# Last expert layer of a graph network on one Trainium2 core: the inner values are kept in DRAM as token rows and gathered, instead of being computed a second time

## The chip, the cores and the metric

The kernel runs on one core of a Trainium2 chip. The metric is the time of one execution in microseconds (us). Three runs of the kernel before the change took 1784.53, 1791.91 and 1784.44 us; their median is 1784.53 us. One further execution was taken with the profiler.

The core has five engines, and the text calls them by their short names: TensorE (PE, with its weight loads as PEld), VectorE (DVE), ScalarE (ACT), GpSimd (POOL) and SyncE (SP). Each works through its own list of instructions in order, and semaphores tie the lists together. SP, ACT and POOL issue the transfers between DRAM and the on-chip memory (SBUF); TensorE writes its results into another on-chip memory (PSUM), from which DVE or ACT must copy them out.

## What is computed

The model has two layers over 2500 nodes (tokens) with 256 features. Each layer adds a graph convolution, an attention block and a layer of experts. Only the last part of the second layer changes, a layer of eight experts of which each token uses the one that its gate likes best:

```python
def _L1_ffn_ref(x, W1, b1, Wg, bg, Wd, bd):
    xf = x.reshape(-1, orig_shape[-1])
    H = jax.nn.gelu(xf @ W1 + b1, approximate=False)        # 2500 x 1024
    probs = jax.nn.softmax((H @ Wg + bg) / TEMP, axis=-1)   # 2500 x 8
    assign = jnp.argmax(probs, axis=-1)
    out = jnp.zeros_like(xf)
    for e in range(Wd.shape[0]):
        y = H @ Wd[e] + bd[e]                               # 1024 -> 256
        sel = (assign == e)[:, None]
        out = out + jnp.where(sel, probs[:, e:e + 1] * y, 0.0)
    return out.reshape(orig_shape)
...
x = x + _L1_ffn_ref(_layernorm(x, axis=-1)[None], L1_ffn_W1, L1_ffn_b1, L1_ffn_Wg, ...)[0]
```

The inner values `H` are the same for all experts: they depend on the token alone. They are needed twice, once for the gate and once for the product with the down weights `Wd[e]` of the token's expert.

## The kernel before

All arithmetic is in float32. The trace shows two instructions of TensorE for each float32 product in the text, and one for each transpose. The 2500 tokens are 20 tiles of `P` = 125, in `NG` = 5 groups of `GT` = 4 tiles (`GC` = 500 tokens). `X` holds the rows on chip; a row has `RW` = 260 numbers: 256 features, then the mean and the inverse deviation of its norm (columns `D` and `D + 1`), the gate's probability (`D + 2`) and the token's number (`D + 3`).

**Gating** (`layernorm_T` at L1899 with `gates`, L1838) goes over the five groups. DVE normalises four tiles into `lnt`, TensorE turns them (L482, eight transposes a group), and the copies of `evacuate` (L98), which alternate between ACT and DVE, put them into `xTf`. For each of eight slices `j` of 128 inner values, TensorE multiplies with `w1` (L1851, four instructions of 500 columns) and ACT applies GELU (L1854) into `h`, one of eight buffers. `logits` multiplies four slices at a time with the gate's weights (L1845). `route` (L1866) turns the logits into probabilities, chooses the expert, and counts where each token's row goes in a sorted table in DRAM; POOL then scatters the rows into `sorted1` and, for the first three groups, also into `early1` (L547, one indirect DMA a tile, by addresses in `to`). `route` is a generator, and its two later parts run within the next group, after slices 2 and 5. The inner values `h` of a group are dropped when the logits are done.

At the head of this stage SP loads the gate's weights and the down weights `wd` of all experts, eight loads of 1 MB (L1733).

**The first four tiles** are full tiles of experts that are known after three groups. `whole_tiles` (L1757) finds them, SP loads their rows from `early1` into `xe` (L1793), DVE normalises them (`turned_first`, L1795), and `hidden_first` (L1802) computes their inner values with the same product and GELU (L1808, L1809) into `he`, while the last group's routing ends. `visit_first` (L1813) multiplies with the down weights.

**The visits** take the other 2000 tokens, in 16 tiles of 128 sorted rows (the last has 80). A tile may hold tokens of several experts, and so there are `NV` = 23 visits, one for each pair of a tile and an expert. `visits` (L620) computes the lists that say which tile and which expert a visit has; they are read into registers at run time. The 16 tiles are handled in groups of 2, 2, 4, 4 and 4:

- `fetch` (L1950) has POOL gather the rows of each tile from `sorted1` into `xs` (L1953; `xs` is `X`, used again), by addresses in `whence`.
- `turned` (L1958) normalises a group's rows a second time on DVE (L1965, `xh`), turns them on TensorE (L1967, `px`), and copies them into `xc`.
- `inner` (L1973) multiplies with `w1` a second time (L1978) and applies GELU on ACT (L1980, and L1983 for the last, short tile) into `hs`, a ring of `RING` = 12 tiles.
- `take` (L1985) copies a visit's tile out of the ring on DVE (L1990), its place being known only at run time.
- `visit` (L1993) multiplies it with the expert's down weights, 16 instructions of 256 columns (L2000, into `py`, of which there are two), makes the list of output rows (L2004, L2005), adds bias, probability and the residual row (L2007, L2008, into `yo`), and has POOL scatter the rows into the output (L1831, in `written`). It reads its row of `xs` at an index from a register (`ds(r, 1)`).

The framework derives what an instruction must wait for from the regions that instructions read and write, in the order of the text; a region at a run-time index counts as the whole. It also fixes each engine's order when the kernel is built, near to the order of the text but not equal to it.

Products in progress take their PSUM tiles from `mm_tile` (L86, four of them). `weights` (L682) hands out tiles of 128x2048 from `wpool`, which has two (L1164); `w1` is one of them.

Of the kernel before, what the change touches and what calls it, by code (L numbers as in the profile page):

```python
# [66 lines left out]
def gps_kernel(ctx: ExitStack, tc: tile.TileContext, a, out):  # L67
# [30 lines left out]
    def evacuate(dst, src):  # L98

        flip[0] ^= 1  # L100
        if flip[0]:
            S.copy(dst, src)  # L102
        else:
            V.tensor_copy(dst, src)
# [602 lines left out]
    early1 = dram.tile([NE // 2 * N, RW], F32, name="early1")  # L707

# [1003 lines left out]
    with ExitStack() as last:  # L1712
# [82 lines left out]
        def turned_first():  # L1795

            t = fin2.tile([P, GT, D], F32, tag="lnt", name="lnt")
            for k in range(GT):
                V.tensor_scalar(t[:, k, :], xe[:, k, :D], xe[:, k, D:D + 1], xe[:, k, D + 1:D + 2], ALU.subtract, ALU.mult)
            transpose_group(xT, 0, lambda k: t[:, k, :])  # L1800

        def hidden_first():  # L1802

            next(routing[-1])
            for j in range(nj):
                ps = mm_tile(128, GC)
                for c in range(2):
                    T.matmul(ps, w1[:, c, j * 128:(j + 1) * 128], xT[:, c, 0:GC], start=(c == 0), stop=(c == 1))  # L1808
                S.activation(he[:, j, :], ps, AF.Gelu, bias=b1f[:, j:j + 1])  # L1809
                if j == 3:  # L1810
                    next(routing[-1])
# [26 lines left out]
        def gates(g):  # L1838
# [9 lines left out]
            for j in range(nj):  # L1848
# [5 lines left out]
                S.activation(hh[j], ps, AF.Gelu, bias=b1f[:, j:j + 1])  # L1854
                if j == 5:
                    logits(0)
# [37 lines left out]
        def sort_all():  # L1894
            V.tensor_copy(fill1, begin1.rearrange("p k t -> p (k t)"))
            moved.append([])
            moved1.append([])
            routing.clear()
            layernorm_T(X, xT, lambda g: fin2.tile([P, GT, D], F32, tag="lnt", name="lnt"), stats=with_row, then=gates)  # L1899
            hidden_first()  # L1900
# [41 lines left out]
        groups = []  # L1942
        for n in (2, 2, 4, 4, 4):
            lo = groups[-1][1] if groups else 0
            groups.append((lo, lo + n))
# [4 lines left out]
        def fetch(lo, hi):  # L1950
            for t in range(lo, hi):
                m = rows_of(t)
                G.indirect_dma_start(  # L1953
                    out=xs[:m, t, :], out_offset=None, in_=sorted1,
                    in_offset=bass.IndirectOffsetOnAxis(ap=whence[:m, t:t + 1], axis=0),
                )

        def turned(lo, hi):  # L1958

            xc = fin2.tile([128, 2, 4 * TS], F32, tag="xc", name="xc")  # L1960
            ps = [psum2.tile([128, 4 * TS], F32, tag="ag", name="px") for c in range(2)]
            for t in range(lo, hi):
                m = rows_of(t)
                xh = fin2.tile([128, D], F32, tag="xh", name="xh", bufs=4)
                V.tensor_scalar(xh[:m], xs[:m, t, :D], xs[:m, t, D:D + 1], xs[:m, t, D + 1:D + 2], ALU.subtract, ALU.mult)  # L1965
                for c in range(2):
                    T.transpose(ps[c][:, (t - lo) * TS:(t - lo) * TS + m], xh[:m, c * 128:(c + 1) * 128], ident[:m, :m])  # L1967
            n = min(hi * TS, LATER) - lo * TS
            for c in range(2):
                evacuate(xc[:, c, :n], ps[c][:, :n])  # L1970
            return xc, n

        def inner(lo, hi, xc, n):  # L1973
            s = lo % RING
            for j in range(nj):
                ps = mm_tile(128, 4 * TS)
                for c in range(2):
                    T.matmul(ps[:, :n], w1[:, c, j * 128:(j + 1) * 128], xc[:, c, :n], start=(c == 0), stop=(c == 1))  # L1978
                k = n // TS
                S.activation(hs[:, s:s + k, j * TS:(j + 1) * TS], ps[:, :k * TS].rearrange("p (k t) -> p k t", t=TS), AF.Gelu,  # L1980
                             bias=b1f[:, j:j + 1])
                if n % TS:
                    S.activation(hs[:, s + k, j * TS:j * TS + n % TS], ps[:, k * TS:n], AF.Gelu, bias=b1f[:, j:j + 1])  # L1983
# [27 lines left out]
        fetch(*groups[0])  # L2011
        fetch(*groups[1])
# [81 lines left out]
```

## Time and profile before

| What | us |
|---|---|
| median of three runs | 1784.53 |
| the profiled execution's own time | 1791.08 |
| its span, from first to last instruction | 1789.4 |
| granted TensorE clock in it, mean | 0.98 |
| L1851, products of gating, begin | 1517.06 |
| one group of gating, from the products of one (1574.63) to those of the next (1593.42) | 18.8 |
| L1822, products of the first four tiles | 1628.01 to 1642.06 |
| L2000, products of the visits, end | 1784.01 |

An execution's time is a little longer than its span, here by 1.7 us. "Busy" is time in which an engine had an instruction under way. In a timeline, a line gives the start, the length, the engine, the line of the kernel, the operation, what it writes and reads, its shape, and how many instructions are merged in it; in brackets stands the idle time of the engine just before it, and what ended it. The modelled end of a TensorE instruction lies after the start of the next one, so its pace is read from the differences of starts. A windows line gives a stretch's start and end, its length, the busy time of PE, PEld, DVE, ACT and POOL with their instructions, the granted clock, the share of the DMA engines' time and the bytes moved in GB/s.

### The profile page before, as it was taken

How to read it: one execution, taken by the hardware profiler on the slowest of the kernel's cores; microseconds unless marked ns; L12 is line 12 of the kernel's file. 1: busy time of each engine (PE TensorE's matmuls, PEld its weight loads, DVE VectorE, ACT ScalarE, POOL GpSimd, SP SyncE). 2: the span in 40 equal slices, each digit the busy share in tenths (PEclk: the TensorE clock that was granted, in tenths of full speed). 3: DMA queues.
4: the chain of work that ended last, by engine and by line, in shares of the span. 5: the costliest groups of instructions: out<-in, count | busy, mean ns of one | idle time of the engine just before them, and what ended most of it. 6: DMA issues, size and time to landing. Idle time of an engine off the chain costs nothing. (4 is left out here: it accounts for less than half of the span.)

```text
span 1789.4 us, 24685 instructions
## 1 busy us (share of the span) xinstructions
PE 1709.2 (96%) x8081; PEld 1252.7 (70%) x8081; DVE 1011.2 (57%) x2909; ACT 654.4 (37%) x1170; POOL 947.7 (53%) x942
## 2 busy tenths in 40 slices
PE   4889998999899999999999999999999999998998
PEld 3656666989778667687776787767877767446767
DVE  7677743434555567577567276575665646234323
ACT  5743322323541434343433524334434331442220
POOL 2003474456207777777774657777777610243222
PEclk7899998999899999999999999999999999999999
DMA  5121147868537534555444764545543312521100
GB/s 143 42 77 37 35 139 244 252 216 236 138 89 183 98 92 112 153 159 172 126 124 118 199 110 146 139 126 152 160 138 97 86 51 75 185 60 48 34 20 29
DMA packets 131653, 216.59 MB, mean 121 GB/s; under 512 B 32832, under 2 KB 97526, under 8 KB 131259
## 3 DMA queue, kind: packets, MB, share of 16 engines
q0 software_dynamic: 51264, 111.78, 23.1%
q1 hardware_dynamic: 77947, 99.17, 18.5%
q10 hardware_dynamic: 2304, 3.94, 0.9%
q8 instruction: 70, 1.15, 0.3%
q14 instruction: 68, 0.56, 0.1%
HBM read 169.44 MB, written 47.79 MB: 121 GB/s over the span
## 5 line engine op out<-in xcount | busy, mean ns | idle before, releaser
L1321 POOL DMA_INDIRECT piece<-tab,nbr x574 | 595.4, 1037 | 188.1 <-issue 155.5
L1638 PE MATMUL mm<-w,h 128*125 128x256 f32 x1280 | 288.8, 379 | 2.0 <-ACT h L1630 1.9
L1627 PE MATMUL mm<-xT,w 128*128 128x500 f32 x640 | 282.1, 582 | 0.0
L1638 PEld LDWEIGHTS mm<-w,h 128*125 128x125 f32 x1280 | 237.7, 188 | 46.3 <-issue 8.5
L1627 PEld LDWEIGHTS mm<-xT,w 128*128 128x128 f32 x640 | 119.1, 190 | 111.0 <-issue 104.3
L1630 ACT ACTIVATE h<-mm,bf 128x500 f32<-128x500 f32 x160 | 106.5, 675 | 202.0 <-PE mm L1627 201.7
L1333 DVE TENSOR_TENSOR piece<-piece 128x1024 f32<-128x1024 f32 (+3 forms) x130 | 146.6, 1129 | 20.6 <-DMA piece<-tab,nbr 20.2
L465 PE MATMUL pa<-edges,xb 125*128 125x500 bf16 x600 | 141.0, 387 | 5.5 <-DVEq L961 3.6
L465 PEld LDWEIGHTS <-xb 125*128 125x128 bf16 x600 | 59.3, 102 | 69.9 <-issue 14.0
L1033 POOL DMA_INDIRECT back<-yo,xs x60 | 60.1, 1002 | 85.9 <-DVE yo L1031 43.6
L1640 DVE TENSOR_TENSOR tok<-tok,mm 125x256 f32<-125x256 f32 x80 | 33.4, 418 | 116.4 <-PE mm L1638 116.3
L1595 DVE TENSOR_TENSOR tok<-tok,po 125x256 f32<-125x256 f32 x80 | 30.1, 417 | 115.4 <-PE po L1592 115.0
L494 ACT ACTIVATE tok<-tok,less,rstd 125x256 f32<-125x256 f32 x140 | 72.1, 590 | 56.3 <-DVE less L492 56.3
L1016 PE MATMUL mm<-xc,wt 128*128 128x128 f32 x688 | 86.9, 281 | 5.5 <-DVE xc L1007 5.5
L811 ACT CAST edges<-mm 125x500 bf16<-125x500 f32 x100 | 65.0, 790 | 71.4 <-PE mm L808 71.4
L1020 ACT ACTIVATE h<-mm,wt 128x128 f32<-128x128 f32 x172 | 49.2, 367 | 106.0 <-issue 84.9
L1016 PEld LDWEIGHTS mm<-xc,wt 128*128 128x128 f32 x688 | 82.7, 196 | 6.3 <-DVE xc L1007 6.2
L1026 PE MATMUL py<-w,h 128*128 x344 | 84.0, 388 | 0.2 <-ACT h L1020 0.2
L2000 PE MATMUL py<-wd,taken 128*128 x368 | 80.9, 379 | 0.5 <-DVE taken L1990 0.5
L1517 PE MATMUL mm<-wa,xT 128*125 128x256 f32 x320 | 76.9, 394 | 4.6 <-ACT xT L487 3.9
L1289 PE MATMUL da<-t,e 125*125 125x256 f32 x320 | 77.7, 379 | 0.0
L2000 PEld LDWEIGHTS py<-wd,taken 128*128 128x128 f32 x368 | 69.7, 190 | 11.3 <-issue 1.4
(486 smaller groups left out, 2995.9 us busy)
## 6 DMA issues: line engine op xcount, KB each, us to landing
wt<-in_expert_in_dram SPq DMA_DIRECT2D x43, 514.0 KB
sorted<-nothing SPq DMA_DIRECT2D x8, 1269.5 KB
piece<-tab,nbr POOLq DMA_INDIRECT x574, 3.1
e<-adj SPq DMA_DIRECT2D x40, 218.8 KB
w<-in_L_mix_W_dram SPq DMA_DIRECT2D x8, 1024.0 KB
wd<-in_L_ffn_Wd_dram SPq DMA_DIRECT2D x8, 1024.0 KB
t<-tab SPq DMA_DIRECT2D x20, 224.0 KB
adj<-wide SPq DMA_DIRECT2D x20, 218.8 KB
```

What stands on the lines that cost most here:

```text
L465: T.matmul(pa[c], table[:, k, n, c * 128:(c + 1) * 128], edges[:, k, :], start=(k == 0 and n == 0), stop=(k == NT - 1 and n == 2))
L494: S.activation(rows[:, k, :D], src[:, lo + k, :D], AF.Identity, bias=less[:, k:k + 1], scale=rstd[:, k:k + 1])
L1016: T.matmul(ps[:, j * TS:(j + 1) * TS], wt[:, c * F0 + j * 128:c * F0 + (j + 1) * 128], xc[:, c * TS:(c + 1) * TS], start=(c == 0), stop=(c ...
L1026: T.matmul(ps, h[:, j * TS:(j + 1) * TS], w2[:, ds(e, 1), j, :], start=(j == 0), stop=(j == NJ - 1))
L1289: T.matmul(sums[d // 2][:, d % 2, :], e[:, d * P:(d + 1) * P], t[:, k, :], start=(i + k == 0 and d % 2 == 0), stop=(i + k == NT - 1 and d ...
L1321: G.indirect_dma_start(out=t[:, i, :], out_offset=None, in_=tab, in_offset=bass.IndirectOffsetOnAxis(ap=by, axis=0))
L1333: V.tensor_tensor(total[:, :m, :], total[:, :m, :], t[:, :m, :], ALU.add)
L1517: T.matmul(ps[:, k * D:(k + 1) * D], hT[:, c, (i + k) * P:(i + k + 1) * P], wk[:, c, :], start=(c == 0), stop=(c == 1))
L1627: T.matmul(ps, w1[:, c, j * 128:(j + 1) * 128], fT[:, c, g * GC:(g + 1) * GC], start=(c == 0), stop=(c == 1))
L1630: S.activation(h, ps, AF.Gelu, bias=bf[:, l, j:j + 1])
L1638: last["product"] = T.matmul(ps, hh[j][:, k * P:(k + 1) * P], w2[:, j, :], start=(j == 0), stop=(j == nj - 1)).ins
L2000: T.matmul(ps, h[:, j * TS:(j + 1) * TS], wd[:, ds(e, 1), j, :], start=(j == 0), stop=(j == nj - 1))
```

## The change

The inner values that gating computes are not dropped. Four slices at a time (a half, `n`), TensorE turns them back into token rows, one tile of 125 tokens after another (`keep_half`, four transposes into one PSUM tile); ACT or DVE copies them into `hr`, one of three buffers, and SP stores them into a new table `inners` in DRAM, 2500 rows of 1024 numbers. `move` (L92) makes two DMA issues of each store. The tiles to be kept wait in a list, `keeping`, from which one is taken after each GELU of `gates` and of `hidden_first`. To make room, `lnt` and `lT` have one buffer instead of two.

In the visits the second norm, its transposes, the second product with `w1` and the second GELU are gone. A tile's rows are gathered from `sorted1` as before, now one tile at a time; DVE makes the token numbers into integers (`ids`); and with them POOL gathers the tiles' inner values from `inners` (`fetch_inner`, 128 rows of 4 KB, into a half of a `weights` tile). `inner` turns them back with eight transposes, and two copies put them into the ring. The loop runs over visits, with the stages two, four and six tiles ahead, in place of groups.

```diff
+    inners = dram.tile([N, F1], F32, name="inners")
...
-            t = fin2.tile([P, GT, D], F32, tag="lnt", name="lnt")
+            t = fin2.tile([P, GT, D], F32, tag="lnt", name="lnt", bufs=1)
...
+        def keep_half(g, n, k, hh):
+
+            ps = mm_tile(P, 4 * 128)
+            for q in range(4):
+                T.transpose(ps[:, q * 128:(q + 1) * 128], hh[q][:, k * P:(k + 1) * P], ident)
+            hr = fin2.tile([P, 4 * 128], F32, tag="hr", name="hr", bufs=3)
+            evacuate(hr, ps)
+            i = g * GT + k
+            move(nc.sync, inners[i * P:(i + 1) * P, n * 512:(n + 1) * 512], hr)
+
+        keeping = []
+
+        def keep(g, n, hh):
+
+            keeping.extend((g, n, k, hh[4 * n:4 * n + 4]) for k in range(GT))
...
                 S.activation(he[:, j, :], ps, AF.Gelu, bias=b1f[:, j:j + 1])
+                if keeping:
+                    keep_half(*keeping.pop(0))
...
                 S.activation(hh[j], ps, AF.Gelu, bias=b1f[:, j:j + 1])
+                if keeping:
+                    keep_half(*keeping.pop(0))
+                if j == 3:
+                    keep(g, 0, hh)
...
             logits(1)
+            keep(g, 1, hh)
             routing.append(route(g, pl))
...
-            lT = fin2.tile([128, GC], F32, tag="lT", name="lT")
+            lT = fin2.tile([128, GC], F32, tag="lT", name="lT", bufs=1)
...
-        def turned(lo, hi):
-
-            xc = fin2.tile([128, 2, 4 * TS], F32, tag="xc", name="xc")
...
-        def inner(lo, hi, xc, n):
...
+        ids = fin.tile([128, NX], I32, name="ids")
+        kept_rows = []
...
+        def fetch(t):
+            m = rows_of(t)
+            G.indirect_dma_start(
+                out=xs[:m, t, :], out_offset=None, in_=sorted1,
+                in_offset=bass.IndirectOffsetOnAxis(ap=whence[:m, t:t + 1], axis=0),
+            )
+            V.tensor_copy(ids[:m, t:t + 1], xs[:m, t, D + 3:D + 4])
+
+        def fetch_inner(t):
+            m = rows_of(t)
+            if t % 2 == 0:
+                kept_rows.append(weights("kept"))
+            h = kept_rows[-1][:, t % 2 * F1:(t % 2 + 1) * F1]
+            G.indirect_dma_start(
+                out=h[:m], out_offset=None, in_=inners,
+                in_offset=bass.IndirectOffsetOnAxis(ap=ids[:m, t:t + 1], axis=0),
+            )
+
+        def inner(t):
+            m = rows_of(t)
+            h = kept_rows[t // 2][:, t % 2 * F1:(t % 2 + 1) * F1]
+            for n in range(2):
                 ps = mm_tile(128, 4 * TS)
+                for q in range(4):
+                    j = 4 * n + q
+                    T.transpose(ps[:, q * TS:q * TS + m], h[:m, j * 128:(j + 1) * 128], ident[:m, :m])
+                to, of = (v.rearrange("p (q t) -> p q t", t=TS)[:, :, :m]
+                          for v in (hs[:, t % RING, n * 4 * TS:(n + 1) * 4 * TS], ps))
+                evacuate(to, of)
...
-        fetch(*groups[0])
-        fetch(*groups[1])
+        for t in range(4):
+            fetch(t)
+        for t in range(2):
+            fetch_inner(t)
         visit_first()
...
-        xc, n = turned(*groups[0])
...
-        for u, (lo, hi) in enumerate(groups):
-            inner(lo, hi, xc, n)
-
-            for v in range(lo, hi if u + 1 < len(groups) else NV):
-                nxt_v = take(v)
-                if taken is not None:
-                    visit(*taken)
-                taken = nxt_v
-                if v == lo and u + 1 < len(groups):
-                    xc, n = turned(*groups[u + 1])
-            if u + 2 < len(groups):
-                fetch(*groups[u + 2])
+        for t in range(2):
+            fetch_inner(t + 2)
+            fetch(t + 4)
+            inner(t)
+        for v in range(NV):
+            nxt_v = take(v)
+            if taken is not None:
+                visit(*taken)
+            taken = nxt_v
+            if v + 2 < NX:
+                inner(v + 2)
+            if v + 4 < NX:
+                fetch_inner(v + 4)
+            if v + 6 < NX:
+                fetch(v + 6)
         visit(*taken)
```

More of the change, by code (lines that the diff above doesn't have):

```diff
@@ L1898, in sort_all @@
             routing.clear()
-            layernorm_T(X, xT, lambda g: fin2.tile([P, GT, D], F32, tag="lnt", name="lnt"), stats=with_row, then=gates)
+            layernorm_T(X, xT, lambda g: fin2.tile([P, GT, D], F32, tag="lnt", name="lnt", bufs=1), stats=with_row, then=gates)
             hidden_first()
@@ L1941, in gps_kernel @@
         xs = whole
[L1942 to L1945, printed above, removed]
+        ids = fin.tile([128, NX], I32, name="ids")
+        kept_rows = []
         def rows_of(t):
             return min(TS, LATER - t * TS)
[L1950 to L1956, printed above, removed]
@@ L1958, in turned @@
-        def turned(lo, hi):
-            xc = fin2.tile([128, 2, 4 * TS], F32, tag="xc", name="xc")
[L1961 to L1971, printed above, removed]
@@ L1973, in inner @@
-        def inner(lo, hi, xc, n):
-            s = lo % RING
-            for j in range(nj):
-                ps = mm_tile(128, 4 * TS)
[L1977 to L1983, printed above, removed]
+        def fetch(t):
[5 more added lines that the diff above has]
+            V.tensor_copy(ids[:m, t:t + 1], xs[:m, t, D + 3:D + 4])
```

## The prediction

> **What bounds the kernel now.** I read the busy shares first, then the last stage by windows, then TensorE alone in order of time, then who waits for whom there, then the few rows that price the new operations. The stage that changes runs from 1514 us to the end at 1789.4: gating until about 1628, the four first tiles until 1642.06, and then the 23 visits.
>
> ```profile
> PE 1709.2 (96%) x8081; PEld 1252.7 (70%) x8081; DVE 1011.2 (57%) x2909; ACT 654.4 (37%) x1170; POOL 947.7 (53%) x942
> ...
> 1580.00:1600.00 20.00, 20.00 (x72) 9.07 (x71) 6.59 (x42) 9.93 (x14) 10.41 (x10) 1.00 0.23 60
> ...
> 1740.00:1760.00 20.00, 20.00 (x89) 16.64 (x88) 6.86 (x14) 1.89 (x6) 3.91 (x4) 1.00 0.06 21
> ```
>
> The window rows (length, busy PE, PEld, DVE, ACT, POOL, clock, DMA share, GB/s) say that TensorE is never idle in the middle of gating nor late in the visits, while DVE and ACT are half idle and the DMA engines nearly so. So TensorE work counts in full, in gating and in the visits alike, and copies and transfers count only where they make it wait. The stretch to be shortened, TensorE alone:
>
> ```profile
> 1644.97 7.17 PE L1978 MATMUL mm<-xc,w1f 128*128 128x256 f32 x32 [0.47 <-ACT xc L102]
> ...
> 1673.15 13.90 PE L1978 MATMUL mm<-xc,w1f 128*128 128x512 f32 x32
> 1686.88 3.62 PE L2000 MATMUL py<-wd,taken 128*128 x16
> 1690.33 1.04 PE L1967 MATMUL px<-ident,xh 128*128 128x128 f32 x8
> 1691.21 10.53 PE L2000 MATMUL py<-wd,taken 128*128 x48
> ...
> 1742.41 41.60 PE L2000 MATMUL py<-wd,taken 128*128 x192
> ```
>
> Ends are modelled, so I take differences of starts. A visit is 16 instructions, 41.6/12 = 3.47 us. Eight transposes start 0.88 us ahead of the next work (1690.33 to 1691.21): 0.11 each. In gating eight of them take 1572.93 to 1573.84, 0.114 each. From 1642.06 to TensorE's last product at 1784.01 are 141.95 us: 23 visits 79.7, L1978 53.9 (7.0, 7.0, 13.7, 13.7, 12.5), turning with its waits 7.0, and 1.2 of waiting ahead.
>
> **Removed.** L1978's 53.9 and the turning's 7.0, that is 61.0 us of TensorE. The 48 GELU instructions of L1980 and L1983 (25.8 us of ACT) and the 16 of L1965 (6.5 us of DVE) go too; they lie beside matmuls, so nothing is counted for them.
>
> **Added on TensorE.** Gating: 5 groups x 2 halves x 4 token tiles x 4 = 160 transposes x 0.114 = 18.2 us, all exposed. Visits: 16 tiles x 8 = 128 x 0.11 = 14.1 us. Balance of TensorE alone: 18.2 + 14.1 - 61.0 = -28.7 us.
>
> A page of the Trainium skill speaks against the change here: "TensorE: Matmul & The Clock Gate", section "Part 4: PE-mode transpose", gives about 275 ns for a transpose inside a kernel. The trace's mean for one transpose is also 275 ns, but from start to end; their pace is 0.114. At 275 ns each, 288 would cost 79 us and the change would lose 46; the pace of the starts decides, so I keep 32.3.
>
> **Evacuations.** 40 new copies of 125x512 in gating, half on ACT (0.57, row L102) and half on DVE (0.68, row L104), 4 of each in a group. TensorE's group grows from 18.8 (1574.63 to 1593.42) to 22.4 us; ACT has 10 busy in 20 now and gets 2.3 more, DVE 2.7 more. They are hidden by the products, which take 1.68 us a slice (4 x 0.42); without that cover, they would cost 25 us. In the visits 32 copies replace the 16 GELUs and the xc copies: hidden by 3.47 us of products.
>
> **The writing out (SP).** 40 stores are 80 DMA issues at about 0.35 us on SP's queue, 256 KB per pair, three hr buffers. SP is not free at the start:
>
> ```profile
> 1518.59 16.43 SPq L1733 DMA_DIRECT2D wd<-in_L_ffn_Wd_dram  x7
> ...
> 1536.00:1540.00 4.00, 4.00 (x19) 2.48 (x18) 3.26 (x14) 3.04 (x5) 0.00 (x0) 1.00 1.09 348
> 1540.00:1544.00 4.00, 4.00 (x11) 1.85 (x10) 0.69 (x4) 2.28 (x4) 0.00 (x0) 1.00 0.52 164
> ```
>
> The expert weights are issued until 1535.0 and move at 348 GB/s until about 1542. The first hr is full near 1528.7; its store queues behind them and lands near 1544. The fourth copy, on DVE near 1535.5, has no buffer until then, and behind it on DVE waits the xTf copy for which the next group's products wait: they would start near 1545.5 instead of 1538.9. Bounds 1 us (if DVE's order puts that copy first) to 6.6; I take 5. Later, SP waits 4.0 us for the early rows and spends 4.93 on the xe loads (L1793); three buffers cover 3 x 2.13 (1.68 + 0.46) = 6.4 us less about 3 of landing: 0 to 5, I take 1.5. DVE's L1799 waits 6.8 us for xe, and copies now queue behind it: 0 to 4, I take 1. One more us for smaller frictions (0 to 1). Gating thus costs 18.2 + 8.5 = 26.7 us (19 to 35).
>
> **The gathers (POOL).** An indirect DMA of 128 rows occupies POOL 0.96 us plus 0.3. No row shows rows of 4 KB. 125 rows of 1252 B cost 1.22 and of 1024 B 1.21, so size hardly tells; bounds 0.95 and four times that, 3.8, with which POOL's turn (scatter, fetch, gather) would be 1.3 + 1.3 + 4.1 = 6.7 us; I take 1.0. Landing: 2.7 us for 133 KB (range below), and 524 KB would need at most 1.5 more at 348 GB/s, so 2.7 to 4.2; I take 3.8. "DMA: Bandwidth & Descriptors", section "Anatomy of one DMA — SWDGE (gpsimd) path", has 2.0 us plus bytes over 436 GB/s, which is an estimate of 3.2; as fetch_inner runs two visits ahead, either figure gives the same sum.
>
> **The new wait.** A visit reads its row of xs at an index known only at run time, so it depends on every fetch written ahead of it, and each fetch on every earlier such read:
>
> ```profile
> 1661.16 0.99 POOL L1953 DMA_INDIRECT X<-sorted,whence  x1 [0.31 <-issue]
> ...
> 1664.98 0.95 POOL L1953 DMA_INDIRECT X<-sorted,whence  x1 [0.30 <-issue]
> ...
> 1667.73 0.16 DVE L2005 TENSOR_TENSOR idx<-far,X 128x1 int32<-128x1 f32 x1 [0.95 <-DMA X<-sorted,whence]
> ...
> 1671.18 0.48 DVE L2008 SCALAR_TENSOR_TENSOR yo<-yo,X 128x256 f32<-128x256 f32 x1
> 1671.94 1.01 POOL L1831 DMA_INDIRECT out_dram<-yo,idx  x1 [6.01 <-DVE yo L2008]
> ...
> DMA to landing us min/median/max: 2.5/2.7/2.8
> ```
>
> At 1667.73 a visit to one of the first tiles waits for the fetch of tiles 4 to 7. Before, that closed three times, once per group. Now fetch stands in every turn of the loop, nine times between visits: L2008 ends, 0.28 to the scatter, 1.32 for it, 2.7 for the fetch to land, then ids 0.2, L2005 0.2, L2007 0.45, L2008 0.5 behind one another on DVE: 5.65 us, where TensorE needs 3.47 + 0.88 = 4.35. On DVE the next take and the evacuation stand behind them, and the next visit waits for that take. Bounds: 4.35 (the loop fits) and 5.65 + 1.3 (fetch_inner between scatter and fetch on POOL) + 1.5 (its bytes ahead of the fetch's) = 8.45. I take 5.65, the trace's own order.
>
> Start of the visits: POOL's four fetches end at 1640.82 as now; the first fetch_inner then lands about 1645, and up to fetch(6) POOL has three scatters of the first tiles and eight gathers to issue, about 15 us, so the first L2008 comes near 1658. Nine loops bring it to 1708.8; take and copy 1.5, then twelve visits 41.6 and three inner 2.6 end TensorE at 1754.5. That is 112.4 us for 141.95: a gain of 29.5 (good end: first L2008 at 1654, loop 5.2, gain 37.6; bad end: 1660, loop 7, gain 15).
>
> **Sum.** +26.7 - 29.5 = -2.8 us; against the profiled execution, 1791.08 (span 1789.4), 1788.3. The profiled run is near the slowest of the three shown, and I carry the difference to their median: 1784.5 - 2.8 = about 1781.5. About 0.5%, 9 us, is what a measurement of this kernel can tell from no change, so my forecast is no measurable change, own range 1776 to 1793.
>
> **Rivals.** *TensorE decides alone* (faster): the loop fits behind the products and the store's wait is reordered away. For: ACT, DVE and DMA are half idle, and only 5.65 against 4.35 stands in the way. Against: the idx wait above. Gating 20, tail 93.8 + 8 = 102, gain 40: -20, 1764.5. *The fetch loop sets the pace* (slower): POOL's order puts fetch_inner between scatter and fetch, and its bytes delay the landing. For: that is the order in the text. Against: it is ready a turn earlier, and an engine's order need not be the text's (four L1978 stand at 1652.97 ahead of the first visit at 1653.94). At 8.45 us a loop nine turns add 25 us to the sum: +22, 1807. It breaks even at 5.65 + 2.8/9 = 6.0 us and passes 0.5% at 7.0. *The stores stall gating at every group*, not only at the weights: 5 x 4 us on top, 1800; against it, 256 KB per 2.13 us is 120 GB/s beside 60, a third of the 348 seen.
>
> **How the numbers follow.** Forecast 0.37, faster 0.36 (TensorE alone, or in part), slower 0.27 (loop 0.20, stores 0.07). The range takes the good and bad ends: 1764 to 1803.
>
> **What would show it.** In the changed profile: 160 transposes in gating at a pace near 0.114; the gap ahead of the second group's products (5 us right, 1 wrong); L2008 to L2008 in the first ten visits 5 to 6 us apart, then 3.5; idx or ids waiting for X from sorted each turn; fetch_inner near 1.0 us of POOL. I am wrong if the loop is under 5 or over 7 us, or if 4 KB rows cost POOL several us.

## The result and the profile after

The kernel after takes 1790.82 us (median of 20 runs, 1782.04 to 1794.91); the kernel before takes 1785.34 beside it (20 runs, 1778.81 to 1791.91). The ratio is 1.0027, 95% interval [1.0017, 1.0038]: 3 to 7 us slower. The forecast was 2.8 us less, too little to be told from no change; measured is a small loss, and the interval excludes no change.

The two profiled executions cannot be compared by their spans (1789.4 before, 1785.0 after): up to gating they hold the same instructions, and that part alone took 13 us less in the profile after. (Of the experiments below one profile, E9's, is of a slow run, 2114.48 us beside a median of 2098.52, and only its turn is read.) So I compare the last stage from its own start, the first transpose of gating (L482 on `lnt`), in three parts: gating until the first tiles' products begin, those products, and the tail from their end to the end of TensorE's last product.

| Part, us | before | after | difference | predicted |
|---|---|---|---|---|
| gating | 112.8 (1515.18 to 1628.01) | 137.8 (1502.32 to 1640.09) | +24.9 | +26.7 |
| first tiles | 14.05 | 15.74 | +1.7 | 0 |
| tail | 141.95 | 122.9 | -19.1 | -29.5 |
| sum | 268.8 | 276.4 | +7.5 | -2.8 |

(The 7.5 us are of one execution each; the medians of the runs differ by 5.5.) First TensorE alone in order of time, where each group of gating begins with its transposes of `lnt`. In the kernel before these stand at 1515.18, 1535.34, 1554.13, 1572.93, 1591.72 and 1608.73. After:

```profile
1502.32 1.31 PE L482 MATMUL mm<-ident,lnt 125*128 125x125 f32 x8 [2.20 <-DVE lnt L506]
1523.78 1.07 PE L482 MATMUL mm<-ident,lnt 125*128 125x125 f32 x8
1549.03 1.07 PE L482 MATMUL mm<-ident,lnt 125*128 125x125 f32 x8
...
1570.84 1.07 PE L482 MATMUL mm<-ident,lnt 125*128 125x125 f32 x8
1592.64 1.07 PE L482 MATMUL mm<-ident,lnt 125*128 125x125 f32 x8
1603.01 0.40 PE L528 MATMUL ps<-way,below 125*125 125x32 f32 x2 [4.03 <-DVE way L1910]
1619.11 1.02 PE L482 MATMUL mm<-ident,lnt 125*128 125x125 f32 x8
```

An undisturbed group has grown from 18.80 to 21.80 us, 3.0 for 32 transposes, a net price of 0.094 each. Two groups have grown by more: the second, 25.25 (1523.78 to 1549.03), and the fifth, 26.47 for 17.01, with a wait of 4.03 inside. VectorE in order of time shows what each waited for; first the second group, then the fifth:

```profile
1538.68 0.69 DVE L104 COPY hr<-mm 125x512 f32<-125x512 f32 x1 [5.20 <-DMA inners<-hr]
1543.09 0.69 DVE L104 COPY hr<-mm 125x512 f32<-125x512 f32 x1 [3.72 <-DMA inners<-hr]
...
1597.59 0.41 DVE L1800 TENSOR_SCALAR lnt<-xe 125x256 f32<-125x256 f32 x1 [1.80 <-DMA xe<-early]
1598.74 0.41 DVE L1800 TENSOR_SCALAR lnt<-xe 125x256 f32<-125x256 f32 x1 [0.74 <-DMA xe<-early]
1600.58 0.41 DVE L1800 TENSOR_SCALAR lnt<-xe 125x256 f32<-125x256 f32 x1 [1.42 <-DMA xe<-early]
1602.76 0.19 DVE L1910 TENSOR_TENSOR way<-w,sign 125x32 f32<-125x32 f32 x1
```

In the second group the copies into `hr` wait 5.20 and 3.72 us for stores that stand behind the loads of `wd`. In the fifth the norm of the sorted rows (L1800) waits for the loads of `xe`, and behind it on VectorE stands the routing (L1910) for which TensorE then waits at L528.

Now the tail: windows of the kernel after (start and end, length, busy time of PE, PEld, DVE, ACT and POOL with their instructions, granted clock, DMA share, GB/s).

```profile
1640.00:1656.00 16.00, 15.74 (x64) 13.13 (x64) 5.82 (x32) 0.00 (x0) 6.42 (x6) 0.89 0.16 42
1656.00:1669.00 13.00, 5.59 (x24) 4.85 (x25) 4.74 (x14) 1.47 (x3) 9.96 (x11) 0.59 0.70 216
1669.00:1690.00 21.00, 20.03 (x102) 17.20 (x101) 10.61 (x30) 2.63 (x5) 9.56 (x10) 0.93 0.42 128
1690.00:1736.00 46.00, 36.62 (x168) 30.43 (x167) 19.26 (x62) 3.96 (x7) 21.83 (x22) 0.89 0.37 113
1744.00:1779.00 35.00, 34.69 (x162) 30.21 (x160) 14.87 (x31) 0.30 (x1) 9.86 (x10) 1.00 0.09 31
```

Two stretches are not full: 13 us right behind the first tiles, with 5.6 of TensorE at a clock of 0.59, and 46 us of visits with 36.6. In the last window, where nothing is fetched any more, TensorE is full again. One turn of the 46 us, all engines in order of time (L1974 is the fetch, L1978 the cast to `ids`, L2022 `idx`, L2025 the visit's last write of `yo`, L1985 the gather, L2007 the take, L1850 the scatter, L2017 a visit's products):

```profile
1690.35 0.97 POOL L1974 DMA_INDIRECT X<-sorted,whence  x1 [0.30 <-issue]
...
1693.24 0.15 DVE L1978 CAST ids<-X 128x1 int32<-128x1 f32 x1 [3.26 <-DMA X<-sorted,whence]
1693.39 0.16 DVE L2022 TENSOR_TENSOR idx<-far,X 128x1 int32<-128x1 f32 x1
1693.64 0.48 DVE L2025 SCALAR_TENSOR_TENSOR yo<-yo,X 128x256 f32<-128x256 f32 x1
1693.67 0.95 POOL L1985 DMA_INDIRECT kept<-inners,ids  x1 [2.34 <-DVE idx L2022]
1694.08 0.69 DVE L104 COPY hs<-mm 128x512 f32<-128x512 f32 x1
1694.87 0.69 DVE L2007 COPY taken<-hs 128x1024 f32 x1
1694.92 1.53 POOL L1850 DMA_INDIRECT out_dram<-yo,idx  x1 [0.30 <-DVE hs L104]
...
1695.62 3.72 PE L2017 MATMUL py<-wd,taken 128*128 x16 [1.81 <-DVE taken L2007]
...
1696.75 0.98 POOL L1974 DMA_INDIRECT X<-sorted,whence  x1 [0.31 <-DVE yo L2024]
```

To be read from the top: the fetch is out, VectorE stands 3.26 us until it has landed, then makes `ids`, `idx` and `yo`, copies, takes; TensorE starts 0.06 us after the take's end, having waited 1.81; POOL gathers, scatters and only then issues the next fetch. From fetch to fetch are 6.40 us. Over eight turns, the visits' products start at 1683.65 and 1735.51: 51.86/8 = 6.48 us, where TensorE alone needs 4.35.

### The profile page after: what moved, and what is told of

Same layout as the page of the kernel before. It is cut to its first block, busy times and chain, and to the rows that moved or that the text cites. A ratio compares the mean times of both kernels' runs of the same rounds, so it can differ in the third digit from the quotient of the medians.

```text
span 1785.0 us, 25155 instructions
## 1 busy us (share of the span) xinstructions
PE 1687.4 (95%) x8177; PEld 1253.0 (70%) x8177; DVE 1028.1 (58%) x2940; ACT 646.7 (36%) x1153; POOL 963.8 (54%) x958
## 5 line engine op out<-in xcount | busy, mean ns | idle before, releaser
L465 PE MATMUL pa<-edges,xb 125*128 125x500 bf16 x600 | 137.4, 380 | 5.6 <-DVEq L962 3.7
L2017 PE MATMUL py<-wd,taken 128*128 x368 | 89.0, 402 | 10.4 <-DVE taken L2007 10.4
L2017 PEld LDWEIGHTS py<-wd,taken 128*128 128x128 f32 x368 | 73.3, 203 | 23.0 <-DVE taken L2007 12.2
L1870 PE MATMUL mm<-xTf,w1f 128*128 128x500 f32 x160 | 77.7, 614 | 0.6 <-ACT xTf L102 0.6
```

Of the source, the lines that this page charges most:

```text
L465: T.matmul(pa[c], table[:, k, n, c * 128:(c + 1) * 128], edges[:, k, :], start=(k == 0 and n == 0), stop=(k == NT - 1 and n == 2))
L1870: T.matmul(ps, w1[:, c, j * 128:(j + 1) * 128], xT[:, c, g * GC:(g + 1) * GC], start=(c == 0), stop=(c == 1))
L2017: T.matmul(ps, h[:, j * TS:(j + 1) * TS], wd[:, ds(e, 1), j, :], start=(j == 0), stop=(j == nj - 1))
```

## The experiments

The runs before and after, those of E1 to E4, of E5 to E8, of E9 and E10, and of E11 were taken in five groups. The kernel before took 1785, 2056, 1783, 2097 and 2058 us in them, so only ratios to it within a group are compared. The longer times lie ahead of the last stage (gating begins at 1502.32 in the profile after, at 1786.09 in E2's), and the last stage's parts compare directly.

| Kernel | gating | first tiles | tail | sum | ratio to before |
|---|---|---|---|---|---|
| before | 112.8 | 14.05 | 141.95 | 268.8 | 1 |
| after | 137.8 | 15.74 | 122.9 | 276.4 | 1.0027 [1.0017, 1.0038] |
| E1 e1_keep_only | 137.1 | 15.74 | 142.1 | 294.9 | 1.0144 [1.0081, 1.0207] |
| E2 e2_true_reads | 136.7 | 14.05 | 114.0 | 264.8 | 0.9996 [0.9960, 1.0032] |
| E3 e3_early_gather | 137.7 | 15.73 | 125.7 | 279.1 | 1.0029 [0.9993, 1.0065] |
| E4 e4_norm_on_pool | 132.4 | 14.05 | 121.7 | 268.1 | 1.0019 [0.9981, 1.0056] |
| E5 e5_both | 132.1 | 14.05 | 113.0 | 259.1 | 0.9944 [0.9923, 0.9964] |
| E6 e6_gather_in_cover | 136.5 | 14.05 | 122.1 | 272.7 | 1.0032 [1.0018, 1.0046] |
| E7 e7_late_cast | 131.4 | 15.73 | 106.4 | 253.6 | 0.9916 [0.9892, 0.9940] |
| E8 e8_short_start | 132.3 | 14.05 | 106.6 | 252.9 | 0.9909 [0.9891, 0.9928] |
| E9 e9_scatter_behind | 139.7 | 15.73 | 118.8 | 274.2 | 1.0011 [0.9976, 1.0047] |
| E10 e10_before_true_reads | 113.7 | 14.05 | 153.3 | 281.0 | 1.0059 [1.0018, 1.0099] |
| E11 e11_before_in_order | 113.6 | 15.73 | 152.8 | 282.2 | 1.0065 [1.0029, 1.0101] |

My theory when they began: gating's price is as predicted, and the gain is lost to the turn of 6.48 us, which a dependence sets that the computation doesn't need. A visit reads its row of `xs` at a number known only at run time, so it waits for every fetch written ahead of it, though it never reads a tile with a number above its own. The rival: POOL's queue or the gathers' bytes set the turn.

**E1, one half of the change alone.** Gating of after (transposes, copies and stores into `inners`), visits of before; `inners` is written and not read.

```diff
-        for t in range(4):
-            fetch(t)
...
+        fetch(*groups[0])
+        fetch(*groups[1])
```

> Gating as in the changed kernel, with the turning back and the stores, but the visits of before (second norm, second product with w1); nothing reads the stored table. My theory: gating costs what the two profiles show, about 25 us from its first product to the first tiles, 18 of it 160 transposes and the rest waits; so this is 25 us slower than before (ratio 1.014), and the visits take their 142 us. Rival (gating's extra work is mostly hidden and the loss lies in the visits alone): 10 us slower or less (1.006).

Gating takes 137.1 us and the tail 142.1, as before: the sum is 26.1 us above before, the ratio 1.0144. So the two halves can be priced one by one: the writing costs what it costs in the whole change (137.8), and nothing of it reappears in the tail.

**E2, the false dependence removed.** Each fetch of a tile and the two reads of `xs` in visits of a lower number are declared independent.

```diff
+            for v, reads in enumerate(read_by):
+                for r in reads if v < t else ():
+                    tc.declare_no_dep(f, r, reason="a visit reads no tile after its own number")
```

> The changed kernel, with one thing told to the framework: visit v reads no tile of xs after tile v, so that it does not wait for the fetches of later tiles nor they for it. My theory (the false dependence closes a loop of 6.5 us a turn): the turns fall to TensorE's 4.4 us and the kernel gains 12 to 17 us on the changed one (1774 to 1779, ratio to before 0.994 to 0.997). Rival (POOL's three issues a turn, or the 524 KB gathers, set the turn): the turns stay over 6 us, within 4 us of the changed kernel (1787 to 1795, ratio about 1.003).

TensorE in order of time, three visits of E2 one after another, without the transposes between them:

```profile
1975.72 5.35 PE L2022 MATMUL py<-wd,taken 128*128 x16 [5.82 <-DVE taken L2012]
...
1981.79 3.62 PE L2022 MATMUL py<-wd,taken 128*128 x16
...
1986.12 3.62 PE L2022 MATMUL py<-wd,taken 128*128 x16
```

From 1981.79 the visits are 4.33 us apart, without a wait: the tail is 8.9 us shorter, and the dependence was the turn's cause. The ratio, 0.9996, is above the 0.994 to 0.997 expected, and the gain below the 12 to 17 us: the stall of 5.82 us remains. The freed fetches are issued in a row, and VectorE executes their casts in order, ahead of the take; that this is what the stall comes from, E7 tests.

**E3, earlier gathers.** The four fetches and the first four gathers ahead of all scatters of the first tiles.

```diff
-        for t in range(2):
-            fetch_inner(t)
-        visit_first()
+        for t in range(4):
+            fourth = fetch_inner(t)
+        waiting = visit_first()
```

> The changed kernel with another order on POOL at the start of the visits: four fetches, then four gathers of inner values, then the fetches of tiles 4 to 6, and only then the scatters of the first four tiles. My theory (the visits start late because the first gathers and fetch 6 stand behind other issues on POOL): the first visit starts 6 us earlier after the first tiles, TensorE's clock stays higher, and the kernel gains about 8 us on the changed one (1783, ratio 0.998). Rival (the chain of fetch, integer copy and gather is as long as it is, whatever the order): under 3 us gained.

This missed. VectorE and TensorE of E3 around the first visit:

```profile
1942.57 1.94 PE L2001 MATMUL mm<-ident,kept 128*128 128x128 f32 x8 [2.68 <-DMA kept<-inners,ids]
...
1954.19 0.69 DVE L104 COPY hs<-mm 128x512 f32<-128x512 f32 x1 [8.83 <-remote]
...
1955.30 0.69 DVE L2011 COPY taken<-hs 128x1024 f32 x1 [0.30 <-DVE far L2025]
...
1956.05 5.46 PE L2021 MATMUL py<-wd,taken 128*128 x16 [4.05 <-DVE taken L2011]
```

Turning back does begin 2.68 us after the first tiles, not 6.31, but a copy into `hs` waits 8.83 us for something that the trace calls remote, the first take stands behind it, and the tail is 2.8 us longer than after's. What that copy waits for stays open. The nearest candidate is the scatters that E3 put last: the last of them is issued at 1951.54, and in the changed kernel ACT's first copy into `hs` is released by one (`out_dram<-yo,whose`, at 1663.31). But the trace of E3 doesn't name it.

**E4, the norm of `xe` off VectorE.** Four instructions of gating's fifth group go to GpSimd.

```diff
-                V.tensor_scalar(t[:, k, :], xe[:, k, :D], xe[:, k, D:D + 1], xe[:, k, D + 1:D + 2], ALU.subtract, ALU.mult)
+                G.tensor_scalar(t[:, k, :], xe[:, k, :D], xe[:, k, D:D + 1], xe[:, k, D + 1:D + 2], ALU.subtract, ALU.mult)
```

> The changed kernel with the norm of the first four tiles (into lnt, from xe) on GpSimd instead of VectorE. My theory (in the last group of gating VectorE stands waiting for the xe rows, and the routing and the copies behind it keep TensorE waiting 4.0 us and its clock low after): that wait is gone and the kernel gains 4 to 6 us on the changed one (1786, ratio 1.000). Rival (the xe rows are late for everything, and the wait only moves to the products of the first tiles): within 2 us of the changed kernel (ratio 1.003).

TensorE alone, the fifth group of E4:

```profile
1876.86 1.07 PE L482 MATMUL mm<-ident,lnt 125*128 125x125 f32 x8
1883.64 0.30 PE L528 MATMUL ps<-way,below 125*125 125x32 f32 x2
1897.95 1.02 PE L482 MATMUL mm<-ident,lnt 125*128 125x125 f32 x8
```

The wait at L528 is gone and the group takes 21.09 us instead of 26.47: 5.4 us. (The ratio, 1.0019, cannot be told from the changed kernel's 1.0027; the gain is read from the stage.) The 1.7 us that the first tiles are shorter are not this edit's: they come and go between kernels with the same first tiles (the table's column for them, E5 and E7).

**E5, E2's and E4's edits together.**

> The changed kernel with both single edits that shortened its last stage: the norm of the sorted rows xe on GpSimd, and visits told that they read no tile later than their own. Theory (two separate causes): the two gains add up, 8.3 us from gating and the first tiles and 11.6 us from the visits, so the stage from gating's first transpose on takes 276.4 - 19.9 = 256.5 us against 268.8 before, and the ratio to the kernel before is about 0.994 (0.992 to 0.997). Rival (both edits pay for the same idle time, or a TensorE with fewer pauses is granted a lower clock): no more than half is left beyond the better of the two, stage 262 or more, ratio 0.997 to 1.000.

The gains add up: gating 132.1, tail 113.0, ratio 0.9944. This is faster than the kernel before, and shows that they are separate causes. (The 256.5 us expected counted the 1.7 of the first tiles twice.) A stall of 4.68 us is left between the visits.

**E6, the gather moved under the fetch's landing.** The changed kernel, with the dependence in place.

```diff
-            if v + 4 < NX:
-                fetch_inner(v + 4)
             if v + 6 < NX:
-                fetch(v + 6)
+                latest = fetch(v + 6)
+            if v + 4 < NX:
+                with tc.issue_after(latest):
+                    fetch_inner(v + 4)
```

> The changed kernel with one order changed on GpSimd's queue: the gather of tile v+4's inner values is placed directly behind the fetch of tile v+6, and no longer between a fetch's landing and the scatter. Theory (the turn of 6.5 us is a chain of GpSimd's queue and the fetch: fetch 0.97, landing, cast and idx 0.3, gather 1.25, scatter 1.4, next fetch): the gather leaves the chain and runs while the fetch lands, a turn of 5.2 to 5.6 us, so 8 turns give 7 to 10 us; stage 266 to 270 us instead of 276.4, ratio to the kernel before 0.998 to 1.000. Rival (the 524 KB of each gather set the turn, wherever the gather stands): the fetch now lands beside the gather's bytes, later by as much as the gather left the chain; turn 6.3 to 6.6 us, stage 275 to 278, ratio 1.002 to 1.004.

The theory missed: the visits' products start at 1682.48 and 1733.41, eight turns of 6.37 us. One turn of E6:

```profile
1692.38 1.27 POOL L1850 DMA_INDIRECT out_dram<-yo,idx  x1 [2.67 <-DVE yo L2026]
...
1693.95 0.97 POOL L1974 DMA_INDIRECT X<-sorted,whence  x1 [0.31 <-issue]
...
1695.23 0.95 POOL L1986 DMA_INDIRECT kept<-inners,ids  x1 [0.30 <-PE mm L1998]
1696.71 0.15 DVE L1978 CAST ids<-X 128x1 int32<-128x1 f32 x1 [3.06 <-DMA X<-sorted,whence]
...
1697.51 0.42 DVE L2025 TENSOR_TENSOR yo<-py,bdf 128x256 f32<-128x256 f32 x1
1697.97 0.49 DVE L2026 SCALAR_TENSOR_TENSOR yo<-yo,X 128x256 f32<-128x256 f32 x1
1698.38 0.69 DVE L104 COPY hs<-mm 128x512 f32<-128x512 f32 x1
...
1699.53 1.23 POOL L1850 DMA_INDIRECT out_dram<-yo,idx  x1 [3.35 <-DVE hs L104]
```

The gather is now under the landing, and the landing is no later for it: 2.76 us from issue to cast, 2.90 in the mean of nine fetches, beside 3.07 in the changed kernel. So the rival's numbers came out (6.37 us, ratio 1.0032), but not its reason: the bytes do not delay a fetch that lands beside them. What the gather left free, VectorE took. The scatter needs `yo`; in the changed kernel's turn above it followed the end of `yo` by 0.8 us, POOL being at the gather, here mostly by 0.28. But there the last write of `yo` began 0.4 us after the cast, and here 1.26 after it, because the addition of the bias (L2025) now stands behind the cast. Without the gather the chain is still 6.36 us long: 0.28 to the scatter, 1.57 for it with its gap, 2.76 for the fetch and its landing, 1.75 from the cast to the end of `yo`.

**E7, casts out of the way.** E5, with the cast at the gather instead of at the fetch, pinned behind the take.

```diff
+            V.tensor_copy(ids[:m, t:t + 1], xs[:m, t, D + 3:D + 4])
             G.indirect_dma_start(
                 out=h[:m], out_offset=None, in_=inners,
...
-                fetch_inner(v + 4)
+                with tc.issue_after(copied[-1]):
+                    fetch_inner(v + 4)
```

> As e5_both, with the cast of a tile's numbers on VectorE moved from its fetch to its gather, and pinned behind the copy of the visit four tiles ahead. Theory (in e2_true_reads VectorE's casts wait in order for fetches that were issued in a row, and the take behind them comes late: PE waited 5.82 us): that wait goes, the visits run at TensorE's pace from the second on; stage 4 to 7 us less than e5_both, near 251, ratio to the kernel before 0.990 to 0.994. Rival (what was late was not the casts but the inner rows themselves, GpSimd's queue being full in these turns): the wait stays, with the gather as its end; stage as e5_both, ratio 0.994.

TensorE of E7, the one wait that is left in the loop:

```profile
1691.92 1.06 PE L2002 MATMUL mm<-ident,kept 128*128 128x128 f32 x8 [0.99 <-DMA kept<-inners,ids]
1692.82 3.62 PE L2022 MATMUL py<-wd,taken 128*128 x16
```

The tail falls to 106.4 us, 6.6 less than E5's, and no visit waits for a take any more; one wait of 0.99 us, for a gather, is left in the loop. The ratio is 0.9916. Waits for in-order casts were the second cost, the one that E2's edit brings with it.

**E8, two gathers early.** E7, with only the first two gathers ahead of the first tiles' scatters.

```diff
+                with tc.issue_after(second):
+                    written(done[0], idx[:, k:k + 1], yo[:, k, :])
```

> As e7_late_cast, with the first two gathers placed on GpSimd's queue right behind the first four fetches, ahead of the first tiles' scatters. Theory (in the changed kernel the first gather stands 3 us behind its fetch's landing because a scatter and a fifth fetch were ahead of it): turning back begins about 3 us after the first tiles' end instead of 6.3, and the first visit 2 to 4 us earlier; stage 2 to 4 us less than e7_late_cast. Rival (as in e3_early_gather, gathers side by side and the delayed scatters give it back later): the first visit starts no earlier than 12 us after the first tiles' end; stage as e7_late_cast or up to 3 us more.

The start of E8, TensorE alone:

```profile
1655.96 1.94 PE L2003 MATMUL mm<-ident,kept 128*128 128x128 f32 x8 [2.90 <-DMA kept<-inners,ids]
...
1662.82 1.94 PE L2003 MATMUL mm<-ident,kept 128*128 128x128 f32 x8 [2.46 <-DMA kept<-inners,ids]
1664.80 5.64 PE L2023 MATMUL py<-wd,taken 128*128 x16
```

Turning back begins after 2.90 us, and the first visit 11.7 us after the first tiles' end instead of 13.2. But the tail is as long as E7's. The 1.5 us are given back: 0.9 by a wait of 1.91 us for a gather at 1689.67, where E7 waits 0.99, and 0.7 by the first visit, 5.64 us long instead of 4.97. The rival was right about the stage, and missed the first visit by little (11.7 for its 12). E8 and E7 can't be told apart (0.9909 and 0.9916).

**E9, the scatter out of the turn.** The changed kernel, dependence in place, with the scatter behind the next fetch.

```diff
+                latest = fetch(v + 6)
+            if rows is not None:
+                with tc.issue_after(latest):
+                    written(done[1], *rows)
```

> The changed kernel with another order on GpSimd's queue: the scatter of a visit's rows is placed behind the fetch of tile v+6 instead of ahead of it; the false dependence stays. Theory (the turn is one serial chain: yo's end, scatter 1.3 and two gaps of 0.3, fetch and landing 2.8, cast and idx 0.3, VectorE's next yo 1.6): without the scatter in it the chain is 4.8 to 5.3 us, so 8 turns give 9 to 13 us; tail from the first tiles' end 110 to 114 us instead of 122.9, ratio to the kernel before 0.995 to 0.999. Rival (as with the gather in e6_gather_in_cover, something else in the turn fills the time, above all VectorE's queue of cast, copies and take): turn 6.1 us or more, tail 119 to 123, ratio 1.001 to 1.004.

The theory missed: the products of the visits that wait start at 2020.24, 2026.45, 2032.34, 2037.79, 2044.00, 2049.67 and 2057.30, 6.2 us apart in the mean (5.5 to 7.6), and the ratio, 1.0011, is the rival's. POOL of E9, three instructions in order of time:

```profile
2018.43 1.20 POOL L1986 DMA_INDIRECT kept<-inners,ids  x1 [1.77 <-issue]
...
2019.94 1.07 POOL L1974 DMA_INDIRECT X<-sorted,whence  x1 [0.30 <-issue]
...
2021.32 1.02 POOL L1850 DMA_INDIRECT out_dram<-yo,idx  x1 [0.30 <-issue]
```

The scatter has left the chain, but the gather, which waits for the cast, now stands ahead of the fetch and takes its place. In this profile a fetch's landing also takes longer, 3.6 to 3.9 us from issue to cast and once 5.8, where seven of the changed kernel's nine take 2.6 to 3.1; the gather's bytes now go directly ahead of the fetch, but whether they are the reason was not tested. Moving one member lets the next one in; of the edits tried, only E2's opens the chain.

**E10 and E11, the same freedom for the kernel before.** If the old visits gained as much from E2's edit, the change itself would be worth nothing. E10 is the kernel before with that edit; E11 pins the freed fetches behind the first tiles' scatters as well.

```diff
+                with tc.issue_after(done[0][-1].ins):
+                    fetch(*groups[u + 2])
```

> The kernel before with the one edit of e2_true_reads: visits told that they read no tile later than their own. Theory (there a fetch stands between visits only three times, and of the 141.95 us of the tail only 8.2 are turning and waiting, of which 32 transposes at 0.11 are 3.5): it can gain at most 4.7 us; tail 137 to 142 us, ratio 0.997 to 1.000. Rival (the false dependence costs the old visits as much as the new ones, 9 to 12 us, and then the change itself is no better once both are rid of it): tail 130 to 133, ratio 0.993 to 0.995.

> As e10_before_true_reads, with the later fetches pinned on GpSimd's queue behind the scatters of the first tiles. Theory (in e10 the freed fetches were put ahead of those scatters, and ACT's writes of hs waited for them: PE 4.55 and 5.89 us): with the scatters first these two waits go, the tail falls from 153 to 138 to 142 us, the kernel before gains nothing that can be measured from true reads: ratio 0.997 to 1.001. Rival (the wait for hs comes from something else that the freed fetches delay): PE's waits of 4 to 6 us stay, tail 148 or more, ratio 1.004 or more.

Both theories missed, on the slow side: tails of 153.3 and 152.8; E11's tail and ratio are its rival's. ACT and TensorE of E11 at the start of the visits:

```profile
1935.89 0.47 ACT L1985 ACTIVATE hs<-mm,b1f 128x256 f32<-128x256 f32 x1 [4.52 <-remote]
1940.81 0.47 ACT L1985 ACTIVATE hs<-mm,b1f 128x256 f32<-128x256 f32 x1 [4.45 <-remote]
...
1942.68 2.08 PE L1983 MATMUL mm<-xc,w1f 128*128 128x256 f32 x4 [10.82 <-ACT xc L102]
```

The first group's writes of `hs` wait for something remote, and TensorE waits 10.82 us behind them. In E11 the first tiles' scatters had long been issued (the last at 1923.48), so E10's explanation, that the writes wait for these, falls; twelve freed fetches were issued between 1924.97 and 1938.86, but the trace doesn't name what the writes wait for. It stays open, as in E3. What is shown is that this edit, as it stands, makes the old kernel slower. That its visits had nothing to win apart from the start is an estimate (153.3 less E10's two waits of TensorE, 4.55 and 5.89, is 142.9, beside 141.95); an old kernel with true reads and without these waits was not run.

## Why the prediction was wrong

Point by point, by its own steps.

**TensorE's balance held.** 61.0 us of products and turning are gone. The transposes of gating cost 0.094 us each, net, where 0.114 was taken (15.0 us instead of 18.2). Their starts are 0.11 apart, but the second `logits` of a group, which stands behind four of them, takes 1.35 us to the next start (1591.29 to 1592.64) where it took 1.86 before (1571.07 to 1572.93). Those of the visits are at 0.11 (1.04 long, 0.88 to the next start). With the loop's waits taken away but for one (E7) the tail is 106.4 us; the rival "TensorE decides alone" had 102. (At 275 ns a transpose the prediction's sum would have come to about +44; its 46 is the difference of the two prices.)

**Gating came out near by errors that cancel, which is luck.** Predicted +26.7, measured +24.9. The transposes took 3.2 less, and the store's stall at the `wd` loads, which was to cost 5 in bounds of 1 to 6.6, cost 3.4 (25.25 less 21.80). The term that was too small is the one for the `xe` rows, 1.5 on SP and 1 on VectorE, with 1 of friction: the fifth group alone lost 5.4 (E4), because behind L1800 on VectorE stands the routing for which TensorE waits. The bounds given, 0 to 5 and 0 to 4, held it; the values chosen inside them did not. The rival "the stores stall gating at every group" is excluded: the third and fourth groups are at 21.80. The first tiles, put at no change, are 1.7 longer in the profile after; kernels with the same first tiles run them in 14.05 as well (E2, E4, E5, E6, E8), so no run shows this as a price of the change.

**The tail failed, and in it the turn.** In the prediction's own marks, the first L2008 of the visits (L2025 in the changed kernel, the last write of `yo`) was to come 15.9 us after the first tiles' end, nine loops were to take 50.9, and the rest 45.7: 112.4. Measured are 19.1 (to 1674.96), 58.5 (to 1733.45) and 45.2: 122.9. The rest was right; 7.6 us were lost in the nine loops and 3.2 at the start.

*The turn.* "I take 5.65, the trace's own order" is the step that failed. The mechanism, a serial chain through the dependence, was right (E2), and the size wrong. In the mean of the nine turns, from one `yo` to the next (between the visits' products it was 6.48), us:

| Part of the turn | predicted | after | E6 |
|---|---|---|---|
| end of `yo` to the scatter | 0.28 | 0.95 | 0.43 |
| scatter to the next fetch | 1.32 | 1.50 | 1.53 |
| fetch to the cast of its numbers | 2.7 | 3.07 | 2.90 |
| cast to the end of the next `yo` | 1.35 | 0.97 | 1.62 |
| turn | 5.65 | 6.50 | 6.47 |

The largest error is the first. In the changed kernel the gather stands on POOL ahead of the scatter and keeps it from following `yo` at once; "the trace's own order" had no gather, and the prediction named it as a bound and a rival and left it out of the 5.65. Next come the landing (two of the nine took 3.8 and 3.9, and the trace doesn't say why) and POOL's gaps. The rival "The fetch loop sets the pace" named 6.0 us as the point from which it decides, and 6.50 is beyond it. Of its two reasons the gather's place is in the table, but moving it alone is worth nearly nothing (E6), and the bytes delay no fetch that lands beside them (E6; for a fetch issued right behind a gather, E9, it is open).

*The start.* The first gather was to land 3 us after the first tiles' end; TensorE stands 6.31 us for it, and the first visit's products begin 13.2 us after that end. VectorE and POOL of the changed kernel:

```profile
1652.79 0.15 DVE L1978 CAST ids<-X 128x1 int32<-128x1 f32 x1 [2.88 <-DMA X<-sorted,whence]
...
1657.69 0.95 POOL L1985 DMA_INDIRECT kept<-inners,ids  x1 [0.30 <-DVE yo L1843]
```

The gather's numbers are there at 1652.94, and it is issued at 1657.69: one scatter and two fetches stand ahead of it. Then TensorE works at a granted clock of 0.59; eight transposes take 1.94 us, later 1.04, and the first visit 5.08, later 3.62. The prediction counted instructions on POOL, and neither this order nor the clock.

The Trainium skill has a rule that bears on the start: "TensorE: Matmul & The Clock Gate", section "Part 1: The HAM clock gate (the "warmup" mystery)", says that the clock halves after an idle window of about 3.4 us and is full again after as long of work. The 6.31 us pause and the 0.59 behind it agree with the first half. The second is not seen: three times eight transposes, in a row from 1662.14 with waits of 0.54 and 0.73 between, all ran at the slow 1.94 to 1.97 us, and the first visit after them, from 1669.05, was slow in part. E8, whose pause was 2.90 us and whose transposes were just as slow, 1.94 us, shows that staying below that length didn't help here.

The measured time lies between 1764 and 1803 because those ends took in a turn of 7 us (summed from their own terms, the ends come to 1766 and 1804). The loss itself, 0.27%, is below the 0.5% that the prediction took as the bound; 20 runs of each kernel tell it from nothing all the same.

## What to carry to other kernels

When a loop has a transfer in every turn and reads its result at an index known at run time, write the turn out as a chain with every gap, and ask first whether the dependence is real: here it was not, and two declarations took 9 us out of the tail, where moving one instruction within the chain took out 0.8 (E6) or left the ratio at 1.0011 (E9). When transfers are freed, look at what stands in order behind their landing: the casts on VectorE cost 6.6 us more, and in the old kernel the same freedom made the tail 11 us longer. A version that beats both kernels comes from the change, the true reads, the norm of `xe` on GpSimd and casts behind the take: 1768.06 us (1763.75 to 1774.38, 6 runs) beside 1783.34 (17 runs).

## What was not expected of the hardware

- The first tiles' products, 64 instructions of the same shapes, take either 14.05 or 15.73 us, in kernels that don't differ there. The granted clock was 1.00 in E8 and E5 and 0.89 in the changed kernel, 0.90 in E7. The pause ahead of them doesn't choose: it was 2.25 us in the changed kernel and in E5, with either length.
- A gather of 128 rows of 4 KB occupies POOL for 0.95 us, as much as a fetch of 128 rows of 1 KB (0.97), and lands after 4.3 us (4.1 to 5.6), the fetch after 3.1.
- In the changed kernel three pauses within the visits (2.90 us ahead of 1703.12, 2.09 ahead of 1716.09 and 1.98 ahead of 1729.32) were each followed by a visit of 5.19 to 5.41 us instead of 3.72; another of 1.81 us, ahead of 1695.62, was not, nor one of 2.50 in E4, ahead of 1973.47. The loss, 1.69 us (5.41 less 3.72), is the same as that of the first tiles (15.74 less 14.05). So the two may be one effect, and the length of the pause alone doesn't decide it; what does, the runs don't show.
